# A two-layer graph network: the second edge layer's gather buffer in five places freed by thirds, its gathers by pair, and the steps of its loop in another order

## The chip, the core and the metric

The kernel runs on one core of one Trainium2 chip. The metric is the device time of one launch in microseconds (us); lower is better. A core has engines that run their own instruction streams and meet at semaphores: PE (TensorE, matrix products; PEld is its weight load), DVE (VectorE), ACT (ScalarE), POOL (GpSimd) and SP (SyncE). Here POOL issues the indirect gathers and SP the plain transfers. Results of PE go to banks of PSUM; everything else works in SBUF.

## The reference

`x` has 6250 rows of 512 floats, and there are 100,000 edges with `src` and `dst` (sorted by `dst`). Two blocks follow one another: each takes a layer norm and a relu, sends rows along the edges, sums them per destination and adds the result to `x`. The first block is a graph attention layer with 8 heads. The second, which this change is about, is a mean over neighbours:

```python
neigh_sum = segment_sum(x[edge_src], edge_dst, num_segments=n)
neigh_mean = neigh_sum / maximum(deg, 1.0)[:, None]
h = einsum('nd,od->no', x, W_self) + einsum('nd,od->no', neigh_mean, W_neigh) + bias
mu, var = mean and variance of h over its 512 columns
h = (h - mu) * rsqrt(var + 1e-5) * gamma + beta
```

The block's output is `x` (after the first block) plus this `h`, where the `x` inside the layer is relu(layernorm(x)).

## The kernel before

**Windows.** The edges, sorted by destination, are dealt to `NW = 66` windows. A window has two pairs (p = 0 and 1), each pair two quarters (q2 = 0 and 1), and each quarter `T = 3` tiles (j) of 128 edges (the last window has one). One indirect DMA on POOL gathers the 128 source rows of one tile, 128 × 512 floats (256 KB), from `h1_d` in DRAM: 12 gathers per window, 784 in all.

**The sum over destinations.** For each tile, PE multiplies the gathered rows by a one-hot matrix (`OHs`), 64 destinations by 128 edges, and adds the result into a bank of PSUM. `add_up1(k, p, j)` (step A`pj`) does it for the two quarters of one j: matmuls at L1285, gather at L1249. `finish1` (C0, C1; L1292) adds what is carried over from the window before: the last sums of each quarter, split into a high and a low half `chi`, `clo` by DVE (`carry_split`; CS0, CS1; L1311 and L1312), times the selection `cs` (`carry_sel`; SEL; L773). `evac1_` (EV0, EV1) lets ACT copy the finished bank to `ws` (L1302), and SP stores it to `acc1_d`. The banks of the sums come in turn from two tags (`w`, `w`, `s`), three in all, so the sums of a pair begin in the bank that was evacuated three pairs ago.

**The slots.** The nodes' output is made in slots of 128 rows. Of seven windows six carry a slot (48 of them in this loop), one is free of it; the late slots at the end use the free windows for part of their work. A slot goes through the loop in stages, spread over several windows:
- `slot1_load`: SP loads `s0` (the first layer's sums) and `sx` (x).
- `slot1_pre` (PRE): DVE makes the residual x (L1042 to L1045), ACT the norm and relu `hs` (L1378).
- `slot1_sums` (SUMS): SP loads the neighbour sums `sa` back from `acc1_d`, after the stores of the window have landed.
- `slot1_mean` (MEAN): ACT scales `sa` by one over the degree (L1391).
- `slot1_run`, a generator advanced one step at a time: T(hs) and T(sa) are the transposes on PE (L1361, tags `t` and `z`); then ACT and DVE split each transpose into `hi` (L1366) and `lo` (L1367); then twelve matmuls with the self weights (L573), then twelve with the neighbour weights and one with the bias (L573, L1411); then statistics, the Newton steps of the reciprocal root, the norm `o` on ACT (L1428), and on DVE the factor gamma and the residual (L1430 to L1433). `put_out` (PUT) stores the result.

The generator of the window's own slot is called `sl_`, that of the window before `last`, and that of two windows before `ends`; `step` advances one of them by one step.

**What sets the order.** The program text does: each engine executes its instructions in the order in which the loop emits them, and waits for what it needs. In the loop of before the order is written out call by call. On PE a window with a slot runs: T(hs), A00, the self product, A01, the neighbour product and the bias, A02, C0, T(sa), A10, A11, A12, C1. On ACT: EV0, MEAN, the root's steps, the norm `o`, EV1, the two `hi`, `hs`. POOL has only gathers here (and the last steps of two late slots).

**The gather buffer.** `g1` is a pool of five tiles, each for one pair: two quarters by three tiles of 512 floats per partition. A tile comes free as a whole, after the last matmul that reads it. The gathers of window k + 3 are issued at the end of window k's steps; those of windows 0 to 2 before the loop. So the first gather of a pair waits for the last matmul of the pair five before it: pair 1 of window k + 2 for A02 of window k, pair 0 of window k + 3 for A12 of window k.

Of the kernel before, what the change touches and what calls it, by code (L numbers as in the profile page):

```python
# [8 lines left out]
FT = mybir.dt.float32  # L9
FR = mybir.dt.float32r  # L10
# [5 lines left out]
N, D, E, H = 6250, 512, 100000, 8  # L16
NT = 49
# [5 lines left out]
T = 3  # L23
NW = 66
# [20 lines left out]
def gnn_kernel(ctx, tc, x, srcp, dstp, attrp, wt0, b0, wsrc, wdst, wts, wtn, bias1, gamma1, beta1, out):  # L45
    nc = tc.nc
    V, A, G, S, P = nc.vector, nc.scalar, nc.gpsimd, nc.sync, nc.tensor
# [3 lines left out]
    def dram(name, shape, dt=FT):  # L51
        return nc.dram_tensor(name, shape, dt, kind="Internal").ap()
# [6 lines left out]
    h1_d = dram("h1_d", [NP, D])  # L59
# [18 lines left out]
    def step(gen):  # L78
        return next(gen, None)
# [24 lines left out]
    for i in range(2):  # L104
        t_ = con.tile([128, H + 1], FT, name=f"rhsf{i}")
# [3 lines left out]
    for i in range(2):  # L109
        t_ = con.tile([128, T, NQ, H + 1], FT, name=f"ex{i}")  # L110
# [3 lines left out]
    for i in range(6):  # L114
        t_ = con.tile([128, NQ * H], FT, name=f"edb{i}")
# [71 lines left out]
    idx = con.tile([128, NQ, NL], I32, name="idx")  # L187
# [207 lines left out]
    sl = {}  # L395
# [221 lines left out]
    def run(gen):  # L617
        for _ in gen:
            pass
# [32 lines left out]
    for t in range(NT):  # L652
        if t + 3 < NT:
            norm(t + 3)
            g, i = where[t + 3]
# [38 lines left out]
    keep = kp.tile([128, LATES + 1, D], FT, name="keep")  # L694
# [375 lines left out]
    def none():  # L1070
        return iter(())
# [11 lines left out]
    def when(k, f, *a):  # L1083
        if 0 <= k < NW:
            f(k, *a)

    def later(f, end=NW):

        return lambda k, *a: f(k, *a) if 0 < k < end else None
# [11 lines left out]
    def slot(w):  # L1101

        return (SLOT.get(w) if w < NW else tail + w - NW if w - NW < TS else None) if w >= 0 else None
# [14 lines left out]
        A00=(0, add_up, 0, 0), A01=(0, add_up, 0, 1), A02=(0, add_up, 0, 2),  # L1118
        A10=(0, add_up, 1, 0), A11=(0, add_up, 1, 1), A12=(0, add_up, 1, 2), C0=(0, finish, 0), C1=(0, finish, 1),
        EV0=(0, evac0), EV1=(-1, evac1), OH=(4, onehot), CS=(0, later(carry_sel)))  # L1120
# [12 lines left out]
    last = none()  # L1133
    ROW = {}
    for k in range(-4, NW + 1):
        sl_ = slot_run(slot(k - 3)) if slot(k - 3) is not None and slot(k - 3) not in LATE else none()
        c, kk = divmod(k, CH)
# [18 lines left out]
        last = sl_  # L1156
# [40 lines left out]
    def late_scales(i):  # L1197
        c, mv = late_part(i), lmv[:, i[0]:i[-1] + 1]
        yield from rstd_of(lp, mv[:, :, 1], LATES, "lt", c[:, :, 9], n=len(i))
        V.scalar_tensor_tensor(c[:, :, 10], mv[:, :, 0], -1.0, c[:, :, 9], op0=OP.mult, op1=OP.mult)  # L1200
# [22 lines left out]
    a = late_scales(one)  # L1223
# [16 lines left out]
    lay0.close()  # L1240


    def gather1(k):
        for p in range(2):
            GT[k, p] = g_ = g1.tile([128, 2, T, D], FT, name="g")
            for j in range(njof(k)):
                for q2 in range(2):
                    c = k * T + j
                    G.indirect_dma_start(out=g_[:, q2, j, :], out_offset=None, in_=h1_d[0:NT * 128, :],  # L1249
                                         in_offset=bass.IndirectOffsetOnAxis(ap=idx[:, 2 * p + q2, c:c + 1], axis=0))  # L1250

    lay1 = ExitStack()
    wp1 = ctx.enter_context(tc.tile_pool(name="wp1", bufs=1))
    g1 = lay1.enter_context(tc.tile_pool(name="gp1", bufs=5))
    own1 = wp1.tile([128, LATES, D], FT, name="own1")
    small = lay1.enter_context(tc.tile_pool(name="small1", bufs=5))
    with tc.tile_pool(name="raw1", bufs=1) as tmp:
        raws = [load_weight(tmp, w, n_, S) for w, n_ in ((wts, "ws1"), (wtn, "wn1"))]
        b1_2 = load_rows(tmp, bias1, S)
        gb = wp1.tile([128, 2, D], FT, name="gb")  # L1260
        for i, v in enumerate((gamma1, beta1)):
            S.dma_start(gb[:, i], bass.AP(tensor=v.tensor, offset=v.offset, ap=[[0, 128], [1, D]]))
        for k in range(3):
            gather1(k)
        wsh, wsl = split_weight(wp1, raws[0], "ws1")
        wnh, wnl = split_weight(wp1, raws[1], "wn1")
        rows1 = split_rows(wp1, tmp, b1_2, "b1")
# [169 lines left out]
    def put_out():  # L1437
        for r, o in DONE:
            S.dma_start(out[ds(r, 128), :], o)
        DONE.clear()  # L1440


    NLATE = len(LATE)
    LT = {}
    PIECES = []

    def piece():
        if not PIECES:
            t_ = g1.tile([128, 2, T, D], FT, name="g")
            PIECES.extend(t_[:, j // T, j % T] for j in range(2 * T))  # L1450
        return PIECES.pop(0)

    def late_sums(i):
        s = LATE[i]
        r = S.value_load(tab[0:1, s:s + 1], min_val=0, max_val=NP - 128)
        y, sx = piece(), keep[:, i]
        S.dma_start(y, acc1_d[ds(r, 128), :])
        LT[i] = dict(s=s, r=r, y=y, sx=sx)

# [71 lines left out]
    def at(w, f):  # L1531
        if slot(w) is not None:
            return f(slot(w))
        return none()
# [4 lines left out]
    def early(w, f):  # L1539
        return at(w, f) if slot(w) not in LATE else none()  # L1540

    last, ends = none(), none()
    for k in range(-1, NW - 1):
        if k + 1 in own_at:
            own_load(own_at[k + 1])
        early(k, slot1_load)
        sl_ = own_run(own_at[k]) if k in own_at else early(k - 2, slot1_run)
        pre = early(k, slot1_pre)  # L1550
        when(k - 1, evac1_, 0)
        early(k - 2, slot1_mean)
        step(sl_)
        when(k, add_up1, 0, 0)
        step(ends)
        when(k - 1, carry_split, 0)
        step(last)
        step(ends)
        when(k, add_up1, 0, 1)
        step(ends)  # L1560
        when(k + 1, onehot, 3)
        step(ends)
        step(last)
        step(ends)
        when(k, add_up1, 0, 2)
        step(ends)
        when(k, finish1, 0)
        step(sl_)
        run(ends)
        put_out()  # L1570
        when(k - 1, evac1_, 1)
        early(k - 1, slot1_sums)
        when(k, add_up1, 1, 0)
        when(k - 1, carry_split, 1)
        when(k + 1, carry_sel, FR)
        when(k, add_up1, 1, 1)
        when(k, add_up1, 1, 2)
        step(sl_)
        run(pre)
        when(k, finish1, 1)  # L1580
        step(last)
        last, ends = sl_, last
        if k >= 0:
            when(k + 3, gather1)
    k = NW - 1
    sl_ = early(k - 2, slot1_run)
    evac1_(k - 1, 0)
# [10 lines left out]
    for i in range(NLATE):  # L1598
        late_sums(i)
# [14 lines left out]
    for i in range(-1, NLATE + 4):  # L1614
# [13 lines left out]
        a, b = late_stats(i - 1), late_newton(i - 3)  # L1628
# [146 lines left out]
```

## Time and profile before

| what | value |
|---|---|
| median of 6 runs | 2744.47 us (2742.43 to 2751.25) |
| profiled execution | 2748.2 us, span 2746.4 us |
| mean granted TensorE clock | 0.879 |
| busy in the span | PE 2182.6 us (79%), DVE 1604.6 (58%), ACT 1114.2 (41%), POOL 1711.7 (62%) |
| software queue of the gathers | 414.35 MB, 51.3% of 16 DMA engines |
| plain transfers of SP | 193.97 MB, 21.7% |
| gathers of the second edge layer (L1249) | 784, mean 981 ns, 768.8 us busy |

How to read the profile: it is one execution on the chip. A group of instructions is given by line, engine and operation with its tiles (`out<-in`), its number, its busy time and the mean of one, and then the idle time of that engine just before its instructions with what ended it. "issue" stands where nothing in the profile shows what the engine waited for. "remote" stands for a semaphore whose sender the profile doesn't tell. The granted clock is the part of TensorE's full clock that it was allowed; a rectangle of a view by windows gives the busy time and, in brackets, the number of instructions of each engine, then the granted clock, the DMA engines' busy share, and GB/s.

### The profile page before, as it was taken

To read this page: it belongs to the slowest core of one execution; us is meant where nothing else is said; L and a number is where in the kernel's file an instruction comes from. 1 tells how busy PE (TensorE), PEld (TensorE's weight loads), DVE (VectorE), ACT (ScalarE), POOL (GpSimd) and SP (SyncE) were. 2 spreads that over 40 slices of the span, in tenths; PEclk is the share of its full clock that TensorE was granted. 3 is DMA by queue.
4 is the path that set the end of the run, shared out by engine and by line. 5 is a ranking of instruction groups with operands and counts; after the bars stand their busy time and mean duration, and the time that the engine had idled before them with its cause. 6 is when DMAs were issued, how large, how long until landed. Compare 5 with 4: busy or idle time off the path is not lost.

```text
span 2746.4 us, 35822 instructions
## 1 busy us (share of the span) xinstructions
PE 2182.6 (79%) x9688; PEld 1086.9 (40%) x9688; DVE 1604.6 (58%) x3323; ACT 1114.2 (41%) x3439; POOL 1711.7 (62%) x1679
## 2 busy tenths in 40 slices
PE   7994488878788888888884577887887979788876
PEld 5762244333343344443342133443443434343434
DVE  8886466566767677666766222454544545454556
ACT  5751355556556566556664111222222222222212
POOL 4665566666666666666652666666666666666662
PEclk9996688889998999988987688998998889899987
DMA  6634576787887887888875777777878788788862
GB/s 205 201 110 137 151 210 194 225 246 232 242 237 238 253 239 237 247 235 239 244 226 152 236 222 225 241 245 247 256 241 256 242 251 253 240 254 253 254 203 90
DMA packets 264719, 611.73 MB, mean 223 GB/s; under 512 B 63605, under 2 KB 74373, under 8 KB 264511
## 3 DMA queue, kind: packets, MB, share of 16 engines
q0 software_dynamic: 125440, 414.35, 51.3%
q1 hardware_dynamic: 138494, 193.97, 21.7%
q8 instruction: 79, 1.29, 0.2%
q14 instruction: 130, 1.06, 0.1%
q10 hardware_dynamic: 576, 1.05, 0.1%
HBM read 511.44 MB, written 97.76 MB: 222 GB/s over the span
## 4 chain that ended last, share of the span: by engine, by line
PE 49%; issue 17%; DVE 10%; POOL 9%; DMA 6%; ACT 4%; another core or an unknown queue 2%; SPq 2%; POOLq 0%; DVEq 0%; ACTq 0%
PE ps_w L974 11%; PE ps_w L1285 8%; POOL g L1249 8%; PE ps_b L573 5%; PE ps_s L1285 4%; PE ps_f L573 4%; PE ps_w L985 3%; DMA gbuf<-h_d,idx 3%; PE ps_z L793 2%; DMA g<-h_d,idx 2%; ACT gbuf L961 2%; PE ps_w L1292 2%; DVE gbuf L942 2%; PE ps_t L781 1%
## 5 line engine op out<-in xcount | busy, mean ns | idle before, releaser
L719 POOL DMA_INDIRECT gbuf<-h_d,idx x784 | 765.4, 976 | 438.0 <-issue 185.6
L1249 POOL DMA_INDIRECT g<-h_d,idx x784 | 768.8, 981 | 394.9 <-issue 217.9
L974 PE MATMUL ps_w<-gbuf,oh 128*64 128x512 f32 x1568 | 502.5, 695 | 32.8 <-issue 23.6
L961 ACT ACTIVATE gbuf<-gbuf,aa 128x64 f32<-128x64 f32 x1788 | 451.8, 338 | 1.6 <-DVE aa L882 1.1
L1285 PE MATMUL ps_w<-g,oh 128*64 128x512 f32 x1048 | 325.6, 664 | 110.4 <-issue 54.1
L942 DVE TENSOR_TENSOR gbuf<-gbuf,ps_c 128x1024 f32<-128x1024 f32 x260 | 311.2, 1209 | 0.0
L1285 PEld LDWEIGHTS ps_w<-g,oh 128*64 128x64 f32 x1048 | 75.4, 146 | 260.0 <-issue 245.4
L860 DVE SCALAR_TENSOR_TENSOR et<-ps_b,et 128x192 f32<-128x192 f32 x66 | 23.4, 355 | 263.6 <-issue 210.0
L608 POOL TENSOR_TENSOR pr<-hr,watt 128x1024 f32<-128x1024 f32 x47 | 113.4, 2413 | 91.3 <-DVE hr L606 74.9
L1285 PE MATMUL ps_s<-g,oh 128*64 128x512 f32 x520 | 154.0, 649 | 17.7 <-issue 12.6
L1311 DVE CAST chi<-ws 128x512 fp32r<-128x512 f32 x130 | 56.1, 432 | 184.9 <-issue 155.0
L985 PE MATMUL ps_w<-ws,cs 128*128 128x512 f32 x228 | 142.2, 705 | 5.2 <-issue 5.2
L995 ACT ACTIVATE ws<-ps_w 128x512 f32<-128x512 f32 x132 | 78.2, 593 | 160.1 <-remote 24.5
L974 PEld LDWEIGHTS ps_w<-gbuf,oh 128*64 128x64 f32 x1568 | 94.8, 149 | 102.3 <-issue 79.4
L977 PEld LDWEIGHTS ps_f<-ex,oh 128*64 128x64 f32 x776 | 69.8, 152 | 161.5 <-issue 159.6
L1367 DVE TENSOR_TENSOR lo<-ps_t,hi 128x512 fp32r<-128x512 f32 x55 | 37.7, 686 | 163.7 <-ACT hi L1366 133.9
L977 PEld LDWEIGHTS ps_s<-ex,oh 128*64 128x64 f32 x792 | 67.8, 151 | 151.8 <-issue 150.6
L802 PE MATMUL ps_z<-ident,es 128*32 128x128 f32 x392 | 73.7, 300 | 64.9 <-DVE nx L829 21.6
L762 DVE TENSOR_TENSOR oh<-ps_c,dsr 128x768 f32<-128x768 f32 x130 | 122.5, 943 | 0.1
L793 PE MATMUL ps_z<-oht,edb 128*32 128x384 f32 (+1 forms) x264 | 110.4, 542 | 12.0 <-DVE mf L822 6.5
L1367 DVE TENSOR_TENSOR lo<-ps_z,hi 128x512 fp32r<-128x512 f32 x48 | 33.0, 688 | 147.9 <-issue 115.2
L785 ACT ACTIVATE oht<-ps_t 128x384 f32<-128x384 f32 x132 | 63.4, 480 | 129.8 <-remote 41.8
(395 smaller groups left out, 4078.0 us busy)
## 6 DMA issues: line engine op xcount, KB each, us to landing
sx<-x SPq DMA_DIRECT2D x95, 256.0 KB
acc_d<-ws SPq DMA_DIRECT2D x182, 130.2 KB
acc_d<-ws SPq DMA_DIRECT2D x182, 128.0 KB
h_d<-hr SPq DMA_DIRECT2D x49, 260.0 KB
gbuf<-h_d,idx POOLq DMA_INDIRECT x784
g<-h_d,idx POOLq DMA_INDIRECT x784
sa<-acc_d SPq DMA_DIRECT2D x48, 260.5 KB
s<-acc_d SPq DMA_DIRECT2D x48, 256.0 KB
```

Source lines behind the costliest of these rows:

```text
L573: P.matmul(pt, a_[:, k], w_[:, k], start=not last[0], stop=stop and k == 3 and w_ is whi_ and a_ is lo)
L608: (G if t < NT - 2 else V).tensor_tensor(out=pr, in0=hr[:, None, 0:D].to_broadcast([128, 2, D]), in1=watt, op=OP.mult)
L719: G.indirect_dma_start(out=g_[:, q, j, :], out_offset=None, in_=h0_d, in_offset=bass.IndirectOffsetOnAxis(ap=idx[:, q, c:c + 1], axis=0))
L762: V.tensor_tensor(out=oh.rearrange("p a j b n -> p (a j b) n"), in0=c_iota[:, None, :].to_broadcast([128, 4 * T, M]), in1=dsr[:, k].rearra ...
L793: P.matmul(z[0:NQ * H, 0:n], ed_tile(k, p), oht[:, p, 0:n], start=(p == 0), stop=False, skip_group_check=True)
L942: eng.tensor_tensor(out=x4, in0=x4, in1=(AA if eng is V else A2)[k][:, i, q].unsqueeze(3).to_broadcast([128, 2, H, D // H]), op=OP.mult)
L961: A.activation(x_, x_, AF.Copy, scale=A2[k][:, T - 1, 2 * p + q2, h:h + 1])
L974: P.matmul(w[r, :], oh[:, p, j, q2], g_[:, 2 * p + q2, j, 0:D], start=(j == 0), stop=False, skip_group_check=True)
L977: P.matmul(sv[r, p], oh[:, p, j, q2], ex[:, j, 2 * p + q2], start=(j == 0 and p == 0), stop=False, skip_group_check=True)
L985: P.matmul(w, CS[k][:, p], c[:, p, 0:D], start=False, stop=True, skip_group_check=True)
L1249: G.indirect_dma_start(out=g_[:, q2, j, :], out_offset=None, in_=h1_d[0:NT * 128, :], in_offset=bass.IndirectOffsetOnAxis(ap=idx[:, 2 * p ...
L1285: P.matmul(BK[p][64 * q2:64 * q2 + 64, :], OHs[k][:, p, j, q2], GT[k, p][:, q2, j, :], start=(j == 0), stop=False, skip_group_check=True)
```

## The change

The buffer becomes one ring tile with five places. Pair p of window k takes place (2k + p) mod 5, so the sequence of places stays the same; but each j (a third of a place, two tiles) comes free by itself, as soon as its own two matmuls are done. The two gathers of one j now go q2 = 1 first, then 0. `gather1` is called for one pair: pair 1 of window k + 2 and pair 0 of window k + 3 are two steps (G1, G0). Five pairs are gathered before the loop, in place of six. The late slots' buffers (`PIECES`) become pieces of the ring. The steps of the loop are the same functions, but their order is read from a string. On PE a window with a slot now runs: the self product, A00, A01, A02, T(hs), A10, the neighbour product and the bias, T(sa), A11, A12, C0, C1. On ACT: MEAN, EV0, the root's steps, EV1, `o`, `hs`, the two `hi`. On DVE chi0 and clo0 come after PRE, and chi1 and clo1 after both `lo`. On SP the stores of both pairs go before the out store, and the load of `sa` after it. In the changed kernel's own line numbers what stands after `gather1` is one lower (L1248, L1284).

```diff
-    def gather1(k):
-        for p in range(2):
-            GT[k, p] = g_ = g1.tile([128, 2, T, D], FT, name="g")
-            for j in range(njof(k)):
-                for q2 in range(2):
-                    c = k * T + j
-                    G.indirect_dma_start(out=g_[:, q2, j, :], out_offset=None, in_=h1_d[0:NT * 128, :],
-                                         in_offset=bass.IndirectOffsetOnAxis(ap=idx[:, 2 * p + q2, c:c + 1], axis=0))
+    def gather1(k, p):
+        GT[k, p] = g_ = ring[:, (2 * k + p) % 5]
+        for j in range(njof(k)):
+            for q2 in (1, 0):
+                c = k * T + j
+                G.indirect_dma_start(out=g_[:, q2, j, :], out_offset=None, in_=h1_d[0:NT * 128, :],
+                                     in_offset=bass.IndirectOffsetOnAxis(ap=idx[:, 2 * p + q2, c:c + 1], axis=0))
...
-    g1 = lay1.enter_context(tc.tile_pool(name="gp1", bufs=5))
+    ring = lay1.enter_context(tc.tile_pool(name="gp1", bufs=1)).tile([128, 5, 2, T, D], FT, name="g")
...
-        for k in range(3):
-            gather1(k)
+        for n in range(5):
+            gather1(*divmod(n, 2))
...
-    PIECES = []
-
-    def piece():
-        if not PIECES:
-            t_ = g1.tile([128, 2, T, D], FT, name="g")
-            PIECES.extend(t_[:, j // T, j % T] for j in range(2 * T))
-        return PIECES.pop(0)
+    PIECES = [ring[:, (2 * NW + i // (2 * T)) % 5, i % (2 * T) // T, i % T] for i in range(NLATE)]
...
+    STEPS1 = dict(EV0=(-1, evac1_, 0), CS0=(-1, carry_split, 0), EV1=(-1, evac1_, 1), CS1=(-1, carry_split, 1), OH=(1, onehot, 3),
+                  SEL=(1, carry_sel, FR), C0=(0, finish1, 0), C1=(0, finish1, 1), G0=(3, gather1, 0), G1=(2, gather1, 1))
+    STEPS1.update({f"A{p}{j}": (0, add_up1, p, j) for p in range(2) for j in range(T)})
+    SLOTS1 = dict(MEAN=(-2, slot1_mean), SUMS=(-1, slot1_sums))
+    ORDER1 = """
+    la en MEAN A00 EV0 A01 A02 sl OH A10 la sl A11 en en en A12 EV1 PUT PRE CS0 SUMS SEL sl en en G1 CS1 C0 la C1 G0
+    """.split()
+
     last, ends = none(), none()
     for k in range(-1, NW - 1):
...
-        when(k - 1, evac1_, 0)
-        early(k - 2, slot1_mean)
-        step(sl_)
-        when(k, add_up1, 0, 0)
-        step(ends)
-        when(k - 1, carry_split, 0)
-        step(last)
-        step(ends)
-        when(k, add_up1, 0, 1)
-        step(ends)
-        when(k + 1, onehot, 3)
-        step(ends)
-        step(last)
-        step(ends)
-        when(k, add_up1, 0, 2)
-        step(ends)
-        when(k, finish1, 0)
-        step(sl_)
-        run(ends)
-        put_out()
-        when(k - 1, evac1_, 1)
-        early(k - 1, slot1_sums)
-        when(k, add_up1, 1, 0)
-        when(k - 1, carry_split, 1)
-        when(k + 1, carry_sel, FR)
-        when(k, add_up1, 1, 1)
-        when(k, add_up1, 1, 2)
-        step(sl_)
-        run(pre)
-        when(k, finish1, 1)
-        step(last)
+        for name in ORDER1:
+            if name == "sl":
+                step(sl_)
+            elif name == "la":
+                step(last)
+            elif name == "en":
+                step(ends)
+            elif name == "PUT":
+                run(ends)
+                put_out()
+            elif name == "PRE":
+                run(pre)
+            elif name in SLOTS1:
+                d, f = SLOTS1[name]
+                early(k + d, f)
+            elif k >= 0 or name[0] != "G":
+                d, f, *a = STEPS1[name]
+                when(k + d, f, *a)
         last, ends = sl_, last
-        if k >= 0:
-            when(k + 3, gather1)
```

More of the change, by code (lines that the diff above doesn't have):

```diff
@@ L1455, in late_sums @@
         r = S.value_load(tab[0:1, s:s + 1], min_val=0, max_val=NP - 128)
-        y, sx = piece(), keep[:, i]
+        y, sx = PIECES[i], keep[:, i]
         S.dma_start(y, acc1_d[ds(r, 128), :])
```

## The prediction

> **What bounds the kernel now.** I began with the page: engine shares, the chain that ended last, the costliest groups.
>
> ```profile
> PE 2182.6 (79%) x9688; PEld 1086.9 (40%) x9688; DVE 1604.6 (58%) x3323; ACT 1114.2 (41%) x3439; POOL 1711.7 (62%) x1679
> PE 49%; issue 17%; DVE 10%; POOL 9%; DMA 6%; ACT 4%; another core or an unknown queue 2%; SPq 2%; POOLq 0%; DVEq 0%; ACTq 0%
> L1249 POOL DMA_INDIRECT g<-h_d,idx x784 | 768.8, 981 | 394.9 <-issue 217.9
> L1285 PE MATMUL ps_w<-g,oh 128*64 128x512 f32 x1048 | 325.6, 664 | 110.4 <-issue 54.1
> ```
>
> PE carries the chain, and 17% of it is "issue": time in which an engine waited for nothing the profile shows. The second edge layer runs from about 1510 to 2660 us; the change touches nothing else. It holds 66 windows of up to 12 gathers. So I asked for the waits of POOL and PE in its steady part, 1700 to 2600 us (total, times, longest):
>
> ```profile
> POOL g L1249 <- issue: 169.8, 556, 0.6
> POOL g L1249 <- remote: 50.4, 19, 4.0
> POOL g L1249 <- PE ps_w L1285: 30.0, 8, 6.0
> POOL g L1249 <- PE ps_z L1361: 15.6, 6, 2.8
> ```
>
> ```profile
> PE ps_f L573 <- issue: 42.1, 34, 2.4
> PE ps_w L1285 <- issue: 28.3, 34, 1.6
> PE ps_w L1285 <- DMA g<-h_d,idx: 6.9, 5, 1.6
> ```
>
> PE hardly ever waits for a gather (6.9 us in 900). POOL waits for PE, which has to free a buffer. POOL's timeline shows how (start, duration, the idle time before):
>
> ```profile
> 2023.58 0.96 POOL L1249 DMA_INDIRECT g<-h_d,idx  x1 [0.30 <-issue]
> 2027.30 0.94 POOL L1249 DMA_INDIRECT g<-h_d,idx  x1 [2.76 <-PE ps_z L1361]
> 2028.55 0.95 POOL L1249 DMA_INDIRECT g<-h_d,idx  x1 [0.30 <-issue]
> ...
> 2041.45 0.95 POOL L1249 DMA_INDIRECT g<-h_d,idx  x1 [0.30 <-issue]
> 2045.04 0.94 POOL L1249 DMA_INDIRECT g<-h_d,idx  x1 [2.64 <-PE ps_w L1285]
> ```
>
> Twelve gathers follow each other at 0.95 + 0.30 us; then one pause of about 2.6, the next at 2045.04, and so on. The pause stands always before the first gather of pair 1, never before pair 0, though both wait for PE. Seven windows take 124 us (42 windows from 1871.9 to 2617.7 us: 17.76 us each). Where a window without a slot has put PE ahead, 24 gathers run in one go, and then PE looks like this:
>
> ```profile
> 1994.11 0.40 PE L573 MATMUL ps_f<-wn_wlo,hi 128*128 128x512 f32 x1 [0.45 <-issue]
> 1997.60 0.39 PE L573 MATMUL ps_f<-wn_whi,hi 128*128 128x512 f32 x1 [1.70 <-issue]
> 2002.50 0.59 PE L573 MATMUL ps_f<-wn_whi,lo 128*128 128x512 f32 x1 [2.21 <-issue]
> ```
>
> ```profile
> 1991.00:1997.00 6.00, 3.44 (x13) 1.72 (x10) 0.59 (x1) 0.00 (x0) 4.48 (x6) 1.00 0.77 227
> 1997.00:2009.00 12.00, 4.44 (x8) 1.42 (x8) 2.23 (x4) 1.80 (x3) 5.54 (x6) 0.55 0.70 229
> ```
>
> Products that follow each other at 0.23 us (1993.02, 1993.26) are now 2 us apart with no wait shown; the granted clock (the number after POOL's count) falls to 0.55. It ends once POOL has paused, here at 2009.66 with 5.59 us. So a long run of gathers slows PE; PE then frees buffers late; POOL pauses; PE recovers. POOL and PE hold each other at 17.76 us. (PE alone: a slot window at full speed is some 14.6 us in the timeline, one without a slot 10 to 11.)
>
> **The change, part by part.** The sum is made against the profiled execution: 2748.2 us (span 2746.4 and 1.8 around it), 3.7 us above the median of 2744.47.
>
> *Release by thirds.* A place holds a pair's six gathers. Today its tile comes free after all its matmuls, so pair 1 waits for A02 and pair 0 for A12; afterwards each third waits for its own matmuls. The places stay five, and matmuls and transfers keep their number. POOL gets six PE waits per window in place of two. A wait that is already satisfied costs nothing visible: the first gather of pair 0 carries one now, and its gap is 0.30. One that is not costs about 2.5 − 0.3 = 2.2 us. Bounds: 0 to 6 × 2.2 = 13.2 us per window. Nearest row: in steady windows the release that is fresh at its turn pauses, and the one that is some 5 us older doesn't. In a dense window of the new order A00 to A02 end at some 4.1, 5.0 and 5.9 us after its start, A10 at 7.4, A11 and A12 at 12.4 and 13.3 (counts of matmuls at the present spacing), and a third takes POOL 2.5. If the first third of pair 1 finds its release L us old, the others find theirs L + 1.6, 3.2, 4.2, 1.7 and 3.4 old; once the first has paused, each is 2.2 older. For L of 4 to 8 only the first pauses. I take that: still one pause per steady window, 15.06 + 0.3 (longer gathers) + 2.2 = 17.55 us. Change: 0.
>
> *The long pauses.* After a run of 24 gathers POOL waits 3.7 to 6.5 us (6.50, 5.59, 5.42, 4.00, 5.98, 3.72, 4.72; mean 5.1) for A02, which PE, still slow, reaches after a self product and two other steps. With thirds it needs A00 only. Least: the 2.5 of a common pause, a gain of 2.6; but the next thirds may then pause too. I take a gain of 1.5 of that 2.6, nearer the full one because later thirds' releases follow within a microsecond. 66 / 7 = 9.4 such places: 9.4 × 1.5 = −14 us. Bounds: −25 and 0.
>
> *Order on PE.* Same instructions. A00 to A02 move ahead of the neighbour product, C0 behind A12. C1 now waits for clo1, which stands on DVE behind lo1, which waits for hi1 and T(sa). From T(sa)'s end, by the mean durations of their groups: hi 0.60, lo 0.69, chi 0.44, clo 0.70 = 2.43 us and four hand-overs; PE has A11, A12 and C0 beside it, 2 × 0.92 (0.91 for two matmuls at 2011.32) + 0.45 = 2.3 us. PE stalls 0.1 us plus the hand-overs: say 0.7 per slot window, 48 of them = 34 us of PE. I put 0 in the sum, since POOL's 17.55 covers PE's 14.6 + 0.7; without that cover it is +34. Bounds: 0 and, if each of the four hand-overs cost half a matmul step, 1.9 × 48 = +91.
>
> *Order on ACT and SP.* The scaling of sa (MEAN) moves ahead of the evacuation of pair 0, so A10, which needs that bank, is queued behind the landing of the sa load. ACT waits for this load today: "ACT sa L1391 <- DMA sa<-acc_d" has 103.3 us in 25 times, 4.1 each. The load is issued on SP behind both stores, whose landing it awaits, and behind the out store, which waits for DVE's last product. By the program it leaves at some 7 us of a window and is wanted at 14.6: covered by about half a window. The evacuation releases nothing that is wanted before 6 us. I take 0; the bounds are 0 and 4.1 × 48 = +197 us, and the lower end wins because the load has half a window where the row's waits come from a scaling asked for early. The residual loads, stores and out store keep their number, and pass each other on SP by one place only.
>
> *chi0 and clo0 late, hi and lo with more room.* DVE's lo waits for hi 112.6 us in 17 times today; both products get a longer lead (8 to 11 us). Off PE's path now, so 0; if the products did wait for them somewhere, a gain of up to 10 us in all, PE having only 16 us on T(sa) and 42 us on products as "issue", most of it slow stretch.
>
> *Before the loop.* Five pairs are gathered in place of six; the sixth waited for the first matmuls anyway: 0. Late slots take pieces of the ring in place of a tile of the pool: same places, 0.
>
> Sum: 2748.2 − 14 = 2734; less 3.7 for the median: **2730 us**, −0.5%.
>
> **A rule weighed.** The row: in the slow stretch PE's gaps are 1.7 to 2.2 us, and the clock is at 0.55 all the same, with products at 0.58 in place of 0.39 us. The Trainium skill, "TensorE: Matmul & The Clock Gate", section "Why this matters for your kernels", asks only for no idle gaps over some 3 us between bursts. By it these stretches would keep their clock, and shortening them would save gaps alone; by the row each also halves the clock. [...]
>
> **The rivals.**
> *Pauses double (slower).* Fresh releases follow one another, and two of six waits pause per window. For it: the kernel's first edge layer, where POOL's waits come in smaller portions, has runs of 3 to 10 gathers, two pauses of 1.2 to 2.1 us, and 18.2 us per window. Against it: each pause makes the following releases older. It decides once L is below 4. At 18.2: 66 × (18.2 − 17.76) = +29, so 2774; at 15.4 + 2 × 2.2 = 19.8 it would be +135, which the gathers' lead of 15 to 35 us over PE would first absorb.
> *PE's new stalls show (slower).* C1 or A10 waits as bounded above; decides where PE's window passes 17.5 us. +34 to +91: about 2790.
> *The long runs go (much faster).* If pauses spread so that no run lasts beyond the 12 to 20 us after which PE slows, seven windows could near POOL's 7 × 15.4 = 108 plus three pauses, 115: 9.4 × 9 = −85, 2660. For it: runs of 12 slow PE by 0 to 3 us only. Against it: what ended runs were the pauses themselves.
> *Nothing.* The gathers are 15 to 35 us ahead as it is; the same pattern returns under another name: 2744.
>
> **How the numbers follow.** About 0.2% (5.5 us) is what a measurement of this kernel can tell from no change. The forecast case, 2715 to 2744, has 0.38 (0.34 of it faster by over 0.2%); the long runs go 0.13; nothing 0.06; doubled pauses 0.24 (0.02 within 0.2%); PE's stalls 0.19 (0.01 or so within). Faster 0.47, same 0.10, slower 0.43. The range leaves out the far ends of the gain and of both losses: 2670 to 2800.
>
> **What would show it.** Right: one pause of about 2.5 us per steady window before the first third of pair 1; the pauses after runs of 24 down from 5.1 to some 3.6; PE's waits for gathers still some 10 us; ACT's wait for sa no longer before T(sa). Wrong: two or more pauses per window with fewer 1.7 to 2.2 us gaps on PE (doubled pauses, or, with a shorter window, the long runs gone); waits of the chi and clo matmuls on DVE, or of A10 on ACT (new stalls). The forecast falls if PE's slow stretches don't depend on how long POOL runs without a pause.

## The result, and the profile after

The changed kernel takes 2762.66 us (median of 19 runs, 2751.71 to 2778.75), beside 2746.84 us for the kernel before (43 runs, 2741.53 to 2759.73). The ratio is 1.0056, with a 95% interval of 1.0045 to 1.0067: slower by half a per cent, or some 16 us. The forecast was 2730 us and faster. The sign was wrong; the range held the time.

The profiled execution has a span of 2763.5 us, 17.1 more than before. Along the program, read from the timelines of both: the first gather of the second layer starts 6.6 us later (1516.9 in place of 1510.3; nothing is changed ahead of it; four kernels that are the same up to there, run on one chip later, differ by 5 us, 1525.1 to 1530.2), the stretch from the first to the last gather's start is 5.7 longer (1157.2 and 1151.5), what follows up to the last matmul of C is 6.7 to 6.8 longer (29.5 after the last gather's end, in place of 22.8), and the tail is 2.0 shorter. So of the change's own 10 us (17.1 less 6.6) 5.7 arise beside the gathers and 6.7 behind the last one, less the 2.0 of the tail. The medians differ by 16 us, so this pair of executions shows some 10 of them.

The page of the changed kernel: busy times, chain, and the group of the gathers.

```profile
PE 2166.0 (78%) x9688; PEld 1110.7 (40%) x9688; DVE 1599.5 (58%) x3323; ACT 1112.0 (40%) x3439; POOL 1705.0 (62%) x1679
PE 48%; issue 18%; DVE 13%; another core or an unknown queue 6%; ACT 5%; DMA 5%; SPq 3%; POOL 2%; ACTq 0%; POOLq 0%; DVEq 0%
L1248 POOL DMA_INDIRECT g<-h_d,idx x784 | 762.7, 973 | 406.9 <-issue 197.2
```

POOL has all but left the chain (9% to 2%), DVE came in (10% to 13%). The waits of PE between 1700 and 2600 us (total, times, longest) say where:

```profile
PE ps_w L1291 <- issue: 48.0, 36, 12.9
PE ps_w L1291 <- DVE chi L1310: 38.0, 10, 9.1
PE ps_s L1291 <- DVE chi L1310: 19.8, 6, 11.0
PE ps_s L1291 <- issue: 18.5, 20, 4.7
...
PE ps_f L573 <- issue: 4.0, 6, 1.0
```

The steps C (L1291; L1292 before) had 8 us of waits in that stretch before, most of them these:

```profile
PE ps_w L1292 <- issue: 4.6, 8, 1.0
PE ps_s L1292 <- issue: 2.6, 4, 1.1
```

Now they have some 130; about half of that has no name, and of the rest nearly all is for `chi`. In return the slow stretches in the products are nearly gone (L573: 42.1 to 4.0 us in the bank that had the most). Over the whole loop behind its first matmul, adding up the gaps above 0.15 us ahead of PE's matmuls, the idle time ahead of C rose from 12.2 to 194.0 us, and the one ahead of everything else fell from 184.2 to 47.8. In all it rose by 45.4. POOL's waits in the same stretch:

```profile
POOL g L1248 <- issue: 152.4, 499, 0.6
POOL g L1248 <- remote: 63.0, 35, 2.9
POOL g L1248 <- PE ps_w L1284: 43.5, 21, 4.0
```

More and shorter ones: pauses above 0.7 us went from 54 to 76 in the loop, those above 3.5 us from 10 to 6.

One window shows how C comes to wait. These are lines of the timelines of SP, ACT, DVE and PE between 2062 and 2084 us (start, duration, instruction, idle time before it):

```profile
2065.63 0.00 SPq L1384 DMA_DIRECT2D sa<-acc_d  x1
```

```profile
2069.77 0.72 ACT L1390 ACTIVATE sa<-sa,slc 128x512 f32<-128x512 f32 x1 [11.26 <-issue]
2070.40 0.58 ACT L1301 ACTIVATE ws<-ps_s 128x512 f32<-128x512 f32 x1
...
2071.21 0.58 ACT L1301 ACTIVATE ws<-ps_w 128x512 f32<-128x512 f32 x1
...
2080.49 0.60 ACT L1365 ACTIVATE hi<-ps_z 128x512 fp32r<-128x512 f32 x1 [6.92 <-remote]
```

```profile
2071.34 0.16 DVE L175 TENSOR_TENSOR s_t<-s_y 128x1 f32<-128x1 f32 x1 [9.20 <-ACT s_y L173]
...
2074.46 0.42 DVE L1310 CAST chi<-ws 128x512 fp32r<-128x512 f32 x1
...
2081.12 0.69 DVE L1366 TENSOR_TENSOR lo<-ps_z,hi 128x512 fp32r<-128x512 f32 x1 [4.52 <-issue]
2081.73 0.42 DVE L1310 CAST chi<-ws 128x512 fp32r<-128x512 f32 x1
```

```profile
2071.03 1.08 PE L1284 MATMUL ps_s<-g,oh 128*64 128x512 f32 x4 [2.67 <-ACT ws L1301]
...
2082.20 0.50 PE L1291 MATMUL ps_s<-chi,cs 128*128 128x512 f32 x1 [3.54 <-DVE chi L1310]
```

SP issues the load of `sa` at 2065.63. MEAN (L1390) is at the head of ACT's queue and has stood there for 11.26 us. Both evacuations (L1301) and the root of the slot two windows back (L173) stand behind it and are done at once when it goes. DVE, 9.20 us idle, then works off the Newton steps, the output, chi0; at 2081.12 it comes to the second `lo`, and only behind it to chi1, which C1 needs: PE starts C1 at 2082.20, 3.54 us late. What MEAN's late start costs PE directly in this window are the 2.67 us ahead of A10, which needs the bank of the late EV0. C1's wait comes from `lo`, which waits 4.52 us for the second `hi`; ACT starts that one, long after T(sa) has ended (2076.1), when a semaphore comes whose sender the profile doesn't tell. So the window shows chi1 behind `lo`; it does not show that MEAN is why `lo` was late.

The whole loop says the same. Follow DVE back from the chi or clo that each wait of C needed to the last instruction that had idle time before it. Of C's 188.0 us of idle time up to the last gather this is `lo` in 154.7, `o` (L1431) in 15.4, and the residual's `sx` (L1045) in 15.1. In the same 188.0 us ACT is idle ahead of `hi` and `hs` for a sender not told in 95.2, and ahead of MEAN in 29.0. What makes `hi` late is open.

In the chain of waits the piece from 2052 to 2066 us lies on SP, which from 2057 on issues at steps of 0.7 us. SP waits 139.2 us in 13 times, up to 16.9, with the residual's load for the DVE instruction of PRE that frees its buffer (L1320 on L1042), and stores and the load of `sa` stand behind that. But such waits are no mark of the loss: between 1700 and 2600 us the residual's load waits for DVE for 80.5 us in the kernel before, for 27.0 in `order_again` below, which has the loss, and for 99.7 in `cs_before_pre`, which has not.

Many of C's waits cost PE twice:

```profile
2168.01 0.49 PE L1291 MATMUL ps_w<-chi,cs 128*128 128x512 f32 x1 [1.27 <-issue]
2168.73 0.50 PE L1291 MATMUL ps_w<-clo,cs 128*128 128x512 f32 x1 [0.23 <-DVE clo L1311]
2169.07 0.58 PE L573 MATMUL ps_f<-ws_whi,hi 128*128 128x512 f32 x1
```

After gaps of 1.27 and 0.23 us the self product, which follows at once in the new order, runs at 0.43 us a step and 0.63 a matmul; later in the same product it is 0.23 and 0.40. Over the 900 us the six groups of the self product are 251.7 us busy, before 215.9. The granted clock is 1.00 from 2160 to 2168 us and 0.52 from 2169.0 to 2172.4: it was halved behind waits that the rule weighed in the prediction (no gaps over some 3 us) would let pass. It is not so behind each wait: of C's 46 waits above 1 us in the loop 33 have such a stretch in the 3.5 us behind them. And the loop as a whole runs at the clock it had (0.90 from 1570 to 2660 us before, 0.89 after), since other slow stretches went.

### The profile page after: what moved, and what is told of

It reads as the page before. It is cut to its first block, busy times and chain, and to the rows that moved or that the text cites. A ratio compares the mean times of both kernels' runs of the same rounds, so it can differ in the third digit from the quotient of the medians.

```text
span 2763.5 us, 36054 instructions
## 1 busy us (share of the span) xinstructions
PE 2166.0 (78%) x9688; PEld 1110.7 (40%) x9688; DVE 1599.5 (58%) x3323; ACT 1112.0 (40%) x3439; POOL 1705.0 (62%) x1679
## 3 DMA queue, kind: packets, MB, share of 16 engines
q8 instruction: 79, 1.29, 0.2%
## 4 chain that ended last, share of the span: by engine, by line
PE 48%; issue 18%; DVE 13%; another core or an unknown queue 6%; ACT 5%; DMA 5%; SPq 3%; POOL 2%; ACTq 0%; POOLq 0%; DVEq 0%
PE ps_w L974 13%; PE ps_w L1284 5%; PE ps_f L573 4%; PE ps_w L985 4%; PE ps_b L573 3%; PE ps_z L793 3%; PE ps_s L1284 2%; ACT gbuf L961 2%; PE ps_t L781 2%; PE ps_z L802 2%; PE ps_w L1291 2%; DVE gbuf L942 1%; DVE hr L613 1%; DMA gbuf<-h_d,idx 1%
## 5 line engine op out<-in xcount | busy, mean ns | idle before, releaser
L1248 POOL DMA_INDIRECT g<-h_d,idx x784 | 762.7, 973 | 406.9 <-issue 197.2
L974 PE MATMUL ps_w<-gbuf,oh 128*64 128x512 f32 x1568 | 509.1, 682 | 37.6 <-issue 26.8
L1284 PE MATMUL ps_w<-g,oh 128*64 128x512 f32 x1048 | 265.2, 616 | 59.9 <-DVE oh L762 45.0
L1284 PE MATMUL ps_s<-g,oh 128*64 128x512 f32 x520 | 137.9, 633 | 21.6 <-issue 15.5
L1291 PE MATMUL ps_w<-chi,cs 128*128 128x512 f32 x86 | 46.6, 542 | 137.1 <-issue 69.4
L1377 ACT ACTIVATE hs<-sx,slc 128x512 f32<-128x512 f32 x45 | 36.7, 815 | 276.8 <-remote 99.3
L995 ACT ACTIVATE ws<-ps_w 128x512 f32<-128x512 f32 x132 | 78.3, 593 | 167.0 <-remote 39.9
L1284 PEld LDWEIGHTS ps_w<-g,oh 128*64 128x64 f32 x1048 | 67.6, 138 | 180.7 <-issue 167.7
L175 DVE TENSOR_TENSOR s_t<-s_y 128x1 f32<-128x1 f32 x103 | 18.0, 175 | 171.7 <-issue 76.8
L1301 ACT ACTIVATE ws<-ps_w 128x512 f32<-128x512 f32 x88 | 51.6, 590 | 149.6 <-remote 42.2
```

What stands on the lines that cost most here:

```text
L974: P.matmul(w[r, :], oh[:, p, j, q2], g_[:, 2 * p + q2, j, 0:D], start=(j == 0), stop=False, skip_group_check=True)
L1284: P.matmul(BK[p][64 * q2:64 * q2 + 64, :], OHs[k][:, p, j, q2], GT[k, p][:, q2, j, :], start=(j == 0), stop=False, skip_group_check=True)
```

## The experiments

Theory A: the new order costs in every window; `chi` comes late to C through ACT, DVE and SP. Theory B: the release by thirds costs, through more pauses. Later came theory C (the loss sits behind the last gather) and theory D (gathers last longer beside DVE's casts).

The runs came from several chips, of two kinds: on two of them the kernel before takes about 2395 us and POOL pauses nowhere, on the others 2745 to 2783 us with the pauses of the profile above. Every ratio is against runs of the kernel before on the same chip at the same time (2779.45 and 2745.80 are one chip at two times). The ratio is the recorded one; the quotient of the two medians differs from it by up to 0.1%.

| run | before there, us | this, us | ratio (95%) |
|---|---|---|---|
| ring_old_order | 2394.96 | 2393.32 | 0.9999 (0.9987 to 1.0011) |
| pool_new_order | 2394.96 | 2405.27 | 1.0054 (1.0033 to 1.0075) |
| ev0_first | 2394.96 | 2403.65 | 1.0043 (1.0029 to 1.0058) |
| cs1_first | 2394.96 | 2403.80 | 1.0044 (1.0027 to 1.0061) |
| after_again | 2393.92 | 2406.91 | 1.0048 (1.0030 to 1.0066) |
| after_beta | 2393.92 | 2395.05 | 1.0011 (0.9999 to 1.0024) |
| before_beta | 2393.92 | 2388.56 | 0.9968 (0.9956 to 0.9980) |
| all_moved | 2393.92 | 2396.99 | 1.0019 (1.0006 to 1.0033) |
| after_beta_twice | 2779.45 | 2797.21 | 1.0062 (1.0034 to 1.0090) |
| before_beta_chi_act | 2779.45 | 2758.63 | 0.9933 (0.9908 to 0.9958) |
| after_beta_chi_act | 2779.45 | 2787.86 | 1.0032 (1.0013 to 1.0051) |
| ring_again | 2782.63 | 2773.02 | 0.9967 (0.9956 to 0.9978) |
| order_again | 2782.63 | 2793.27 | 1.0034 (1.0022 to 1.0046) |
| cs_before_pre | 2782.63 | 2777.04 | 0.9981 (0.9969 to 0.9994) |
| pre_beta_chi | 2782.63 | 2771.60 | 0.9953 (0.9938 to 0.9968) |
| ring_beta_chi | 2745.80 | 2735.31 | 0.9964 (0.9953 to 0.9976) |
| after_once_more | 2745.80 | 2763.76 | 1.0054 (1.0035 to 1.0072) |

### Thirds or order, on a faster chip

`ring_old_order` is the ring with the old loop:

```diff
-            when(k + 3, gather1)
+            when(k + 2, gather1, 1)
+            when(k + 3, gather1, 0)
```

> The ring of five places freed by thirds and the gathers by pair, with the loop's steps in the old order. Theory A (the order costs: C waits for chi behind a chain through ACT and SP): no wait of the C matmuls on chi, and the long runs of 24 gathers gone, so 2715 to 2745 us. Theory B (the thirds cost: more pauses of POOL): two pauses per window in many windows, 2755 to 2770 us.

`pool_new_order` is the new loop with the old pool:

```diff
-        GT[k, p] = g_ = ring[:, (2 * k + p) % 5]
+        GT[k, p] = g_ = g1.tile([128, 2, T, D], FT, name="g")
...
-            for q2 in (1, 0):
+            for q2 in range(2):
```

> The new order of the loop's steps, with the old pool of five tiles that come free as a whole. Theory A: PE's idle time ahead of the C matmuls stays at some 130 us in the steady 900, 2755 to 2775 us. Theory B: as before, 2740 to 2750 us.

`ev0_first` and `cs1_first` are the changed kernel with one step moved:

```diff
-    la en MEAN A00 EV0 A01 A02 sl ...
+    la en A00 EV0 MEAN A01 A02 sl ...
```

> The changed kernel with one step moved: EV0 ahead of MEAN on ACT, so that the evacuation of pair 0 doesn't wait behind the landing of sa. Theory A with ACT's order as its main part: the idle time ahead of the C matmuls falls from 130 to below 70 us in the steady 900, 2720 to 2745 us. With DVE's order as its main part, or by theory B: 2755 to 2770 us.

```diff
-    ... CS0 SUMS SEL sl en en G1 CS1 C0 la C1 G0
+    ... CS0 SUMS SEL CS1 sl en en G1 C0 la C1 G0
```

> The changed kernel with one step moved: chi1 and clo1 ahead of hi and lo on DVE, so that C1 doesn't wait for lo, hi and hs. Theory A with DVE's order as its main part: the idle time ahead of the C matmuls falls below 70 us of the steady 900, 2720 to 2745 us. With ACT's order as its main part (EV1 late behind MEAN): little is gained, 2750 to 2765; by theory B the same.

The ratios of the first two fit theory A: the order is the whole loss, the thirds give nothing (the times expected were for the slower kind). But the mechanism isn't A's here. In the trace of `pool_new_order` C is idle for 12.4 us in the whole loop, and no gather is more than 0.7 us behind the one ahead of it. POOL runs without a pause, 784 times about 1.29 us; it sets the pace and PE waits for gathers. In the profiles `ring_old_order` and this run differ by 14.0 us: 4.9 from first to last gather (1008.2 and 1013.1 us), 5.1 from there to the last C (11.8 and 16.9), and the rest ahead of the loop and in the tail. Behind the last gather the timelines of POOL, DVE and PE of `pool_new_order` read (L1460 is L1461 in the kernel before and L1454 in the changed one):

```profile
2328.14 8.58 POOL L1460 TENSOR_TENSOR keep<-keep,gb 128x512 f32<-128x512 f32 x7
2336.69 1.25 POOL L1429 TENSOR_TENSOR sx<-sx,gb 128x512 f32<-128x512 f32 x1
```

```profile
2327.38 0.69 DVE L1366 TENSOR_TENSOR lo<-ps_z,hi 128x512 fp32r<-128x512 f32 x1 [7.36 <-ACT hi L1365]
2327.99 10.24 DVE L1310 CAST chi<-ws 128x512 fp32r<-128x512 f32 x1
```

```profile
2338.28 0.80 PE L1291 MATMUL ps_w<-chi,cs 128*128 128x512 f32 x1 [9.04 <-DVE chi L1310]
```

A cast that takes 0.42 us elsewhere lasts 10.24, as long as POOL's seven additions of beta for the late slots and the one behind them. PE's C1 waits 9.04 for it. In `ring_old_order` the chi of another C is caught by the same additions (10.14 us), and PE waits 5.54 for it. `ev0_first` and `cs1_first` stand at 1.0043 and 1.0044 beside the 1.0054 of `pool_new_order`, within its interval, so neither move shows a gain here; in `cs1_first` C1's chi is out in time and the next one is caught (5.00 us). That made theory C.

### Behind the last gather

`after_again` is the changed kernel. In `after_beta` and `before_beta` the additions leave POOL for the free windows:

```diff
+        if k in own_at and own_at[k] in LATE:
+            i = LATE.index(own_at[k])
+            V.tensor_tensor(out=keep[:, i], in0=keep[:, i], in1=gb[:, 1], op=OP.add)
...
-    for i in range(NLATE):
-        late_beta(i)
```

> The changed kernel itself, beside the next three on one chip. By both theories 0.4 to 0.7% above the kernel before. Theory C (the loss sits at the loop's end: DVE's chi or sx there lasts as long as POOL's seven additions of beta, and the new order has C1 of the last full window behind it): the last matmul of the loop comes 12 to 17 us after the last gather has started where POOL never pauses, against 5.5 with the old order. Theory A (C waits for chi in every window): the idle time ahead of the C matmuls is spread over the loop.

> The changed kernel with the seven additions of beta taken off POOL behind the last gather, and done on DVE one at a time in the free windows of the loop. Theory C: the 10 us chi is gone and the kernel gains 7 to 11 us on the changed one, so it comes within 0.2% of the kernel before. Theory A: the end gains what it gains, 0 to 3 us, and the windows' waits stay.

> The kernel before with the same move of the seven additions. Theory C: there PE had other work or was at its end beside them, so it gains less than the changed one does, 2 to 6 us. Theory A says nothing of it: 0 to 3 us.

`all_moved` is `after_beta` with both moves of steps, EV0 ahead of MEAN and CS1 ahead of `sl`:

> The changed kernel with EV0 ahead of MEAN, CS1 ahead of hi and lo, and the additions of beta in the free windows. Theory A: both orders count in every window, so this is the best of the four, 0.3% or more below the kernel before. Theory C alone: no better than with the additions moved alone.

The block that theory C names is real on this kind of chip: the changed kernel gains 11.9 us (2406.91 to 2395.05), the one before 5.4 (2393.92 to 2388.56), and the end behind the last gather falls from 17.3 to 7.1 us in the first. But it is only part of the loss. Between the orders 13.0 us become 6.5, by the recorded ratios 0.48% becomes 0.43. Where the rest is was not found: the end differs by 2.5 us (7.1 and 4.6), and the spans of the two profiled executions are the same (2386.6 and 2386.7). `all_moved` gains nothing on top; these moves of steps did not help where POOL sets the pace.

`before_again` is the kernel before once more, one profiled execution of 2765.89 us, on a chip of the slower kind, as are the three beside it. `after_beta_twice` does the additions behind the last gather twice:

```diff
-    for i in range(NLATE):
-        late_beta(i)
+    for i in range(2 * NLATE):
+        late_beta(i % NLATE)
```

> The kernel before itself, for its trace on the chip of these runs. By theory C its DVE has one instruction of 9 to 10 us beside POOL's seven additions, and its loop ends about 5 us after the last gather has started plus what C1 waits for it.

> The changed kernel with the seven additions of beta behind the last gather done twice (so the output counts beta twice in the late slots). Theory C: the DVE instruction beside them lasts some 8.6 us longer, and the kernel takes 7 to 9 us more than the changed one, about 0.8 to 0.9% above the kernel before. If POOL's additions only happened to run beside a wait of another cause: 0 to 2 us more.

Timelines of POOL and DVE of `after_beta_twice`:

```profile
2708.91 17.18 POOL L1454 TENSOR_TENSOR keep<-keep,gb 128x512 f32<-128x512 f32 x14
```

```profile
2710.74 17.12 DVE L1045 TENSOR_TENSOR sx<-sx,s 128x512 f32<-128x512 f32 x1 [3.12 <-DMA sx<-x]
```

The DVE instruction goes along: 17.12 us, in place of 6.26 in the changed kernel's profile, and the end lasts 38.5 us in place of 29.5. So the blocking is real on both kinds, and in the profiles its price at the end is 7 to 9 us per seven additions (`after_once_more`, on the same chip, has 31.1). But the kernel as a whole was slower by 0.6%, hardly more than the change alone on chips of this kind (0.54 and 0.56%), where 0.9% was expected; the runs were too few to tell, and the interval reaches to 0.9. The old order pays for the block too here: `before_again` needs 22.8 us up to the last C, and 13.6 with the additions moved and chi on ACT (`before_beta_chi_act`); the new order needs 29.5 and 21.1. So on these chips the block is no difference between the orders.

### DVE's casts

`before_beta_chi_act` and `after_beta_chi_act` have the additions moved, and chi cast by ACT:

```diff
-        V.tensor_copy(hi, WS[k][:, p])
+        A.activation(hi, WS[k][:, p], AF.Copy)
```

> The kernel before with the additions of beta moved, and chi cast by ACT in place of DVE. Theory D (a gather takes longer while DVE casts chi, which is where the changed order loses its steady 4 to 8 us): of 560 gathers fewer than 50 above 0.98 us in place of 78, and another 5 to 12 us below the version with the additions moved alone. If the casts only stand beside long gathers: the same time within 2 us.

> The changed kernel with the additions moved, and chi cast by ACT. Theory D: it gains more than the old order does from the same edit, since 102 in place of 78 gathers of 560 were long, and the two orders come within 3 us of each other. If the casts have no part: the 6 us between the orders stay.

Theory D fell. Gathers above 0.98 us number 106 of 560 with chi on ACT and 99 in `before_again`: the casts only stand beside long gathers. Neither expectation held for the second run, yet the pair is telling. With the block gone from both, the changed order is 29 us slower (2787.86 and 2758.63), 25 of them between first and last gather (1179.6 and 1154.5 in the profiles), with 219.8 us of idle time ahead of C in the one and 35.6 in the other. On the slower kind the loss is spread over the windows, as theory A has it. The gain of 0.67% of the old version is partly the end's 9.2 us; what part chi has was not separated.

### Thirds or order, on a slower chip

`ring_again` and `order_again` are `ring_old_order` and `pool_new_order` once more.

> Thirds and gathers by pair, old order. If the order is the whole cause on the slower chips too: within 0.3% of the kernel before, PE's idle time ahead of C below 40 us in the loop. If the thirds cost there: 0.4% or more above.

> New order, old pool. If the order is the whole cause: 0.4 to 0.9% above the kernel before; on a slower chip 150 us or more of idle time ahead of C. If thirds and order only cost together: within 0.2%.

`cs_before_pre` moves both carry splits ahead of the residual:

```diff
-    ... A12 EV1 PUT PRE CS0 SUMS SEL sl en en G1 CS1 C0 la C1 G0
+    ... A12 EV1 PUT CS0 CS1 PRE SUMS SEL sl en en G1 C0 la C1 G0
```

> The changed kernel with CS0 and CS1 ahead of PRE, so that chi and clo no longer stand on DVE behind the residual's loads and behind hi and lo. Theory A on a slower chip: the idle time ahead of C falls from 190 to 220 us to below 60, and the kernel comes to 0.4% below to 0.2% above the kernel before. If the wait moves on to hi and lo (the products then wait for lo, whose chain through sx, hs and hi stays): the idle time moves to L573, and the time stays at 0.4 to 0.9% above. On a faster chip: 0.2 to 0.5% above, since the end stays.

`pre_beta_chi` adds to it EV0 ahead of MEAN, the moved additions and chi on ACT:

> The changed kernel with all that was found: EV0 ahead of MEAN, CS0 and CS1 ahead of PRE, beta in the free windows, chi cast by ACT. Theory A: on a slower chip as good as the old order with beta and chi moved (0.67% below the kernel before) or better, 0.5 to 1.5% below. If the order's cost is elsewhere: above the kernel before by 0 to 0.5%.

PE's waits ahead of C, 1700 to 2600 us, in `ring_again` and `order_again`, and ahead of C and of the products in `cs_before_pre`:

```profile
PE ps_w L1291 <- issue: 6.6, 10, 1.8
PE ps_s L1291 <- issue: 5.9, 9, 1.3
```

```profile
PE ps_w L1291 <- DVE chi L1310: 47.4, 9, 14.8
...
PE ps_s L1291 <- DVE chi L1310: 26.6, 4, 11.2
...
PE ps_w L1291 <- issue: 21.1, 13, 9.5
```

```profile
PE ps_f L573 <- ACT hi L1365: 20.8, 5, 11.6
...
PE ps_w L1291 <- issue: 14.2, 17, 2.4
PE ps_s L1291 <- issue: 7.7, 7, 1.6
```

Here the thirds alone gain 0.33%, with 3 pauses above 3.5 us where the two traces of the kernel before have 10 and 11, and the order alone loses 0.34%, with 152.9 us of idle time ahead of C (133.8 of the 144.6 up to the last gather behind `lo`); the sizes are a little off what was expected, the signs are not. Two steps moved on DVE turn the changed kernel, 0.5% slower on other chips of this kind (on this one it was not run), into one 0.19% faster than the kernel before: no wait for chi is left ahead of C, and C's idle time in the loop is 36.4 us. Part of it moved on to `hi` in the products, as the second of the two expectations had it, but the time did not stay. The idle time ahead of everything else is 177.7 us again, where the changed kernel has 47.8; in all PE is idle for 214.1 us here, 190.9 in `ring_again` and 248.3 in `order_again`, and the times stand in the same order. That shows the cause on these chips: the place of the two splits on DVE, behind PRE and behind hi and lo. The two were moved together; the traces put by far the most on chi1 behind `lo`. With all edits it comes to 0.47% below, just short of what was expected. EV0 ahead of MEAN was tried alone only on the faster kind, so how much MEAN's place does on the slower kind stays open.

### Do the parts add up, and the best version

`ring_beta_chi` is the old order with the ring, the moved additions and chi on ACT; `after_once_more` is the changed kernel beside it.

> Old order, the ring freed by thirds, beta's additions in the free windows, chi cast by ACT. If the gains add on a slower chip: 0.33 + 0.67 = 1.0% below the kernel before, at least 0.8%. If thirds and the rest relieve the same waits: 0.5 to 0.7%. On a faster chip, where thirds gave nothing: 0.3 to 0.6% below.

> The whole change beside it. If thirds and order simply add, -0.33 + 0.34 = 0.0, within 0.2% on a slower chip; if the order's waits for chi eat the thirds' gain, 0.3 to 0.7% above. On a faster chip 0.4 to 0.6% above.

They do not add. The whole change is 0.54% above, while its parts were -0.33 and +0.34%, on another chip; C's idle time is 198.8 us with both and 152.9 with the order alone; that the order's wait takes the thirds' gain fits this, but why it is more than a loss of the gain was not tried. `ring_beta_chi`, 0.36% below and so short of both its expectations, beats both kernels, but not `before_beta_chi_act` (0.67% below, on the same chip at another time): where the additions and chi are moved, the thirds add nothing that shows. The best found is the old kernel with the additions moved (0.32% below on the faster kind) and, on the slower kind, with chi on ACT too.

## Why the prediction was wrong, point by point

**What bounds the kernel** was read rightly for chips of this kind: POOL and PE hold each other, long runs of gathers go with slow stretches of PE. It is no property of the kernel alone, though: on the faster kind there are no pauses, and POOL's rate of 1.29 us per gather binds. And "never before pair 0" is a little too strong: of the 54 pauses 51 stand before the first gather of pair 1, two before pair 0.

**Release by thirds, 0, and the long pauses, -14 us.** The sign was right and the size not far: alone 0.33% of 2782.63, some 9 us, and the long pauses are the ones that went. In the changed kernel 48 of the 76 pauses stand before the first third of pair 1, as forecast; with the thirds alone they are spread over all thirds. On the faster kind, which has none, it gave 0.9999.

**Order on PE: "I put 0 in the sum, since POOL's 17.55 covers PE's 14.6 + 0.7".** This step failed, in its price and in its cover. The wait for clo1 was found, but priced from durations that follow each other without a gap, 0.7 us a slot window. The chain in front of it isn't ready when T(sa) ends: C's idle time is 194.0 us, 2.9 per window over 66, with a single wait of 25.9 and, between 1700 and 2600 us, of up to 12.9. The new order puts chi1 and clo1 behind `lo`, and so C1 inherits what `lo` waits for. That wait stood in the profile before, 234.7 of 900 us:

```profile
DVE lo L1367 <- issue: 122.1, 27, 9.5
DVE lo L1367 <- ACT hi L1366: 112.6, 17, 13.9
```

The prediction names the second row further down and puts it off PE's path, where it was until the change moved the splits behind it. Nor was POOL's 17.55 a full cover. Of PE's 45.4 us of added idle time the stretch from first to last gather kept 5.7 in the first pair of profiles; with the additions and chi moved in both orders the new one is 25.1 longer there. That POOL, which waits for PE itself, can't hide what PE loses is argued, not shown by a run of its own.

**Order on ACT and SP: "By the program it leaves at some 7 us of a window and is wanted at 14.6".** In the window shown this is wrong: the load of `sa` goes out 18.8 us after its window's A00 (2046.8 to 2065.6), since SP has waited before and issues slowly; MEAN idles ACT for 11.26 us and holds two evacuations and a root. But the term that was put at 0, A10 behind the evacuation, was close: A10 waits for it once in the 900 us by the waits that have a name, 2.7 us, and ACT's waits ahead of MEAN fell, from 156.5 to 130.1. How much MEAN's place adds to the lateness of `hi` and chi was not shown on this kind of chip.

**chi0 and clo0 late, 0.** Failed as far as the splits go: their place is what `cs_before_pre` undoes, which comes out 0.19% below the kernel before. By the traces chi0's part is small (30.5 of the 188.0 us, behind `o` and `sx`), and chi1 behind `lo` the main one.

**Before the loop and late slots, 0.** Nothing speaks against it; but the work behind the loop has a price that the prediction didn't see: POOL's additions block DVE there, and the new order has C1 of the last full window behind it. On the faster kind moving them takes 11.9 us off the changed kernel and 5.4 off the one before, so it accounts for at most half of the 13 us between them.

**The rivals.** "PE's new stalls show" is what happened, given 0.19, at its named place; its 2790 was too dear by some 27 us, probably because the slow stretches shrank at the same time (idle time ahead of all else from 184.2 to 47.8 us). "Pauses double" was seen in part, 54 to 76, but cost nothing: the thirds alone, with 79, are faster. The chances of the single cases add up to 0.47 faster, 0.13 same and 0.40 slower, not 0.10 and 0.43.

**The rule on gaps.** Where it differs from the row the row was right again: gaps of 1.27 and 0.23 us were followed by 3.4 us at a granted clock of 0.52.

## What to carry to other kernels

A step moved in a loop is not priced by the durations behind it but by the latest time at which its inputs are ready: follow the chain back over all engines, SP's queue and the buffers' releases included, until it closes or reaches something early. An engine that itself waits for the delayed one may be no cover. And place work that splits a carried value ahead of anything on its engine that waits for a load or for another engine.

## What the runs showed of the hardware

POOL's 128x512 additions block some DVE instructions for as long as they follow each other: 10.24 us for a cast of 0.42 beside eight of them, 17.12 us for an addition of 0.69 beside fourteen and one. Not all: in `cs1_first` a `lo`, which reads a bank of PSUM, takes its usual time in the middle of the seven additions (2333.33 to 2341.98):

```profile
2335.97 0.69 DVE L1366 TENSOR_TENSOR lo<-ps_z,hi 128x512 fp32r<-128x512 f32 x1 [9.72 <-ACT hi L1365]
```

The Trainium skill, "SBUF — State Buffer", section "SBUF: two separate sides", says that GpSimd shares a port pair with those DVE operations that run in a 2-port mode or read two operands from SBUF, and that whichever starts first locks it for its whole instruction. The trace agrees on the lock, and shows one thing more: it wasn't passed to the waiting DVE between POOL's instructions.

The same programs ran at two paces, 2395 us and 2745 to 2783. On the faster chips gathers follow at 0.30 us throughout:

```profile
POOL g L1248 <- issue: 129.8, 426, 0.3
```

This is the changed kernel from 1500 to 2250 us there, where no wait of POOL's gathers is longer than 0.3 us. Steps of 0.65 to 0.76 us from one instruction of SP to the next add up to 4.2 us in those 750; in the same kernel's profile on a slower chip they are 163.6 of the 900 from 1700 to 2600 us. What makes the two kinds differ was not found.
